# A whole network on one core: its order is planned anew, with measured durations and a time to landing for each kind of DMA

## The chip, the cores and the metric

The kernel runs on one core of a Trainium2 chip. The time is the device time of one execution in microseconds (us); a profiled execution also has a span, from its first to its last instruction. Engines: PE (TensorE, matrix products), DVE (VectorE), ACT (ScalarE), POOL (GpSimd) and SP (SyncE), which issues all DMAs here.

## What the kernel computes

The input is a batch of 8 images of 32 channels of 256 x 256 points, in fp32. Four layers follow each other; each one adds to x a function of the group-normalised x (16 groups of two channels):

```python
x = x + _L0_conv_ref(_gn(x), L0_conv_conv_w, L0_conv_conv_b)
x = x + _L1_conv_ref(_gn(x), L1_conv_weight)
x = x + _L2_conv_ref(_gn(x), L2_conv_weight, L2_conv_bias)
x = x + _L3_conv_ref(_gn(x), ...)
```

Layer 0 is a 1 x 1 convolution, followed by a depthwise 5 x 5 convolution whose 25 taps per channel are a pooled 5 x 5 picture of that same result. Layer 1 quantises x and w to 8 bits and takes minus the sum of |patch - w| over 32 channels and 3 x 3 places, for each of 32 output channels. Layer 2 is an ordinary 3 x 3 convolution. Layer 3 cuts the image into windows of 8 x 8, normalises over channels, and passes the result through four small networks: k1, k2 and k3 side by side (on three arrangements of the window), their sum through k4. Each of them is

```python
def _fastkan(x, ln_g, ln_b, ws, wb, bb):
    ln = _layernorm(x, ln_g, ln_b)
    basis = jnp.exp(-((ln[..., None] - GRID) / DENOM) ** 2)
    flat = basis.reshape(*basis.shape[:-2], -1)
    return flat @ ws.T + jax.nn.silu(x) @ wb.T + bb
```

with a grid of 8 points: eight squares and eight exponentials of every element.

## The kernel before

**The work.** A tile has 128 partitions: 4 blocks of rows of the image times 32 channels. An image has 8 chunks of 128 x 2048 values (F = 2048).

- `stage0` (layer 0): loads x by chunks for the sums and the pooled picture (the DMA at L821, sums on DVE at L828 to L834, squares on ACT at L721), then takes the taps on PE (L1084 for image 0; `one_block`, L1012, for the other images), and stores x1. A last walk loads x1 (L1144), scales it on ACT (L1151), rounds it on DVE (L1157, L1158) and stores it as bf16 integers q (L1162).
- `stage1` (layer 1): an image goes in two halves; the half's q is loaded into `qh` (L1231). A half has 16 passes of two output channels. A pass needs 18 distances max(q - w, 0) (2 channels x 9 taps) of 128 x 32 x 258 values. DVE makes them (L1186, one instruction for 8256 values), and where ACT is free it makes the first `RA` rows of one or all of it (L1188). They go to one of two buffers `dv`; PE sums each over the channels into `psA` (L1204, 288 products a pass). When a pass is done, ACT evicts psA (the gate, L1283), 256 times in all: 8 images x 2 halves x 16 passes.
- `stage2` (layer 2): 8 chunks; a load of x2 (L1327 to L1340), a normalisation on ACT (L1345), 9 taps on PE (L1362), an eviction on ACT (L1378) and a store of x3 (L1386).
- `stage3` (layer 3): each of 8 chunks goes through four kan passes (`kan`, 256 in all): centring on PE (L678), an eviction (L1458 on ACT or L1463 on DVE), its square (L1466 on ACT or L1467 on DVE), the variance on PE (L1475), logarithm and exponential for the root on ACT (L1488, L1492), broadcasts on PE (L1507), a product on DVE (L1515); then eight squares (L1611 on ACT or L1616 on DVE), eight exponentials on ACT (L1626), eight main products on PE (L678), one product with silu of the input, and an eviction on ACT (L1699). The input and its silu go through HBM to change their arrangement: stores y, yd, sy, syd, sz (L1543; L1548 in eight DMAs), loads at L1567, L1569, L1588 and L1591, the sums oa and od (stored at L1708, loaded at L1658 and L1662, the latter in sixteen DMAs). ACT uses two tables, one for logarithm and exponential, one for silu; a switch is an instruction of its own (L1805).

**What sets the order.** Nothing of it is written out by hand. Each stage calls `plan.add` with an engine, a duration in us, what it reads and writes, and a rank. `Plan.run` (L263) then walks through time like a scheduler: whenever an engine is free it takes, of the tasks whose inputs are ready and whose buffers fit, the one of the lowest rank; distances and their sums on PE are fillers that an engine takes where nothing else is (`fill`, L389; `piece`, L428; on PE, `on_pe` takes them first when enough have queued up). The list in which tasks were taken is then emitted, and each engine works through its part of it strictly in order. So the planner's durations are never executed: they only decide the order of the instructions and which buffer each one gets. On the chip, an instruction waits for what it needs, and all behind it on its engine wait too.

**What the planner takes a DMA to cost.** SP is busy for the task's duration (often 2.0 us, or 0.5 us for a single DMA); its data arrive when one shared mover has moved all kilobytes before them, at 210 KB per us:

```python
busy[e] = now + us
mover = max(mover, now + us) + t.kb / 210.0
t.end = mover
```

A task that reads the data is ready 2.0 us after that (`LAT["SP"]`), a buffer that a DMA has read is free after 0.5 us.

**Constants.** `room()` divides 41,280 words a partition: three places for `si` (operands of stage 3's last products), two for `dv`, small ones, `NX` fixed places of 3072 words for `x0` (chunks of stages 0 and 2), and the rest in one piece, `sb`: 20,992 words, from which everything else takes what it needs (a chunk of stage 3 takes 2048). With NX = 0, x0 comes from sb too, and only while 6400 words (`WIDE_SPARE`) stay free besides; the first tasks of a kan pass leave `SPARE` words free. `IDLE` says per image how long ACT must have been idle before it takes a distance. When all distances are done (`over()`), squares and evictions may go to DVE as well as to ACT (`.other`). `HOLDT` is the number of the exponential that must be done before a kan pass starts its main products in that last part, `SWITCH` the rank that a table switch costs, `SUMS` when a half's sums of q are taken. `TURN`, `L0A`, `L0B`, `L2A`, `L3A` and `L3B` place the steps of the stages among the ranks, by image; layer 1's pass has the rank of its number, so that, for instance, `L3A[b]` says how far into the next image's layer 1 the layer 3 of image b begins.

Of the kernel before, what the change touches and what calls it, by code (L numbers as in the profile page):

```python
# [13 lines left out]
AF = mybir.ActivationFunctionType  # L14
# [55 lines left out]
NX = 0  # L70
NBAS, NSI = 0, 3
TURN = (
    (0.6962, -0.3, -0.2033, 1.3419, 0.9756, -0.0716, 0.0444, 0.123, 0.0689, 0.1702, 0.1109, -0.1569, 0.9648, 0.4157),
    (0.4978, -0.3, -0.0103, 0.9164, 1.1185, -0.0225, 0.0583, 0.81, 0.1545, 0.2437, 0.1558, -0.1941, 0.9648, 1.2236),
# [12 lines left out]
IDLE = (4.0, 2.0, 8.0, 8.0, 1000.0, 16.0, 8.0, 8.0)  # L87
NDV = 2
SPARE = 1792
# [3 lines left out]
HOLDT = 4  # L93
HOLD = 1
SUMS = 1.314
RA = 4
HALVES = 0
SWITCH = 0.006
L0A = (0.5664, -0.1509, 0.3344, 0.396, 0.4459, 0.5225, 0.5225)
L0B = (1.2, 0.9692, 1.0696, 0.2501, 0.4205, 0.2211, 0.5807)  # L100
L2A = (-0.4443, 0.2719, 0.2484, 0.4, -0.0809, 0.0425, 0.3641, 0.335)
L3A = (0.3139, 0.6, 0.5451, 0.5786, -0.4733, 0.6, 0.5806, 0.0117)
L3B = (0.3712, 0.937, 0.2, 0.3674, 0.2077, 0.8294, 0.444, 0.2665)
# [12 lines left out]
NI = 4  # L116
# [21 lines left out]
class Plan:  # L138
# [4 lines left out]
    LAT = {"PE": 0.15, "DVE": 0.14, "ACT": 0.2, "SP": 2.0}  # L143
# [13 lines left out]
    def add(self, eng, us, fn, r=(), w=(), rank=0.0, after=(), table=None, spare=0, kb=0, acc=()):  # L157
        t = Task()
        t.eng, t.us, t.fn, t.rank, t.table, t.spare, t.kb = eng, us, fn, rank, table, spare, kb
        t.n, t.gate, t.other = len(self.tasks), None, None  # L160
# [102 lines left out]
    def run(self):  # L263
# [4 lines left out]
        table, mover = None, 0.0  # L268
        count = 0
# [17 lines left out]
        while left or any(not p.done for p in self.passes):  # L287
            moved = True
            while moved:
                moved = False  # L290
                for e in engines:
# [34 lines left out]
                    if t.table in (LN_EXP, SILU):  # L326
                        if table != t.table:
                            t.load = table = t.table
                            us += 1.29
                    t.start = now  # L330
                    order.append(t)
                    if e == "SP":
                        busy[e] = now + us
                        mover = max(mover, now + us) + t.kb / 210.0
                        t.end = mover
                    else:
                        busy[e] = t.end = now + us
                        if e == "ACT" and t.n is not None:
                            self.idle = t.end
# [7 lines left out]
            while events and events[0][0] <= now + 1e-9:  # L347
# [3 lines left out]
                elif what == 2:  # L351
                    t.over = True
                    left -= t.n is not None
                    heapq.heappush(events, (t.end + (0.5 if t.eng == "SP" else self.LAT[t.eng]), 3, count, t))
# [53 lines left out]
class Pass:  # L408
# [19 lines left out]
    def piece(self, plan, e):  # L428
# [32 lines left out]
        us = (0.13 + 1.075 * (hi - lo) / 16) if e == "DVE" else 0.12 + 3.575 * (hi - lo) / 16  # L461
# [41 lines left out]
def kernel(  # L503
# [180 lines left out]
    class Norm:  # L684
# [23 lines left out]
        def add_squares(self, src, at, i, size, rank, first=None):  # L708

            if not self.chunks & 1 << i:  # L710
                self.chunks |= 1 << i
                plan.add(
                    "DVE", 0.16,
# [6 lines left out]
                "ACT", 0.18 + 0.8365e-3 * size,  # L720
# [7 lines left out]
        def finish(self):  # L728
# [14 lines left out]
            plan.add("DVE", 1.1 if n == 1 else 1.5, first, r=[*self.bufs, self.summed], w=[small], rank=self.rank)  # L743
# [11 lines left out]
            plan.add("DVE", 0.5, second, r=[p], w=[small], rank=self.rank)  # L755
# [22 lines left out]
            plan.add("DVE", 2.8, third, r=[p], w=[small] + out, rank=self.rank)  # L778
# [30 lines left out]
    def stage0(b, rank, span, after):  # L809
# [8 lines left out]
        for k in range(NCH):  # L818
            xt = Buf("x0", XW)
            plan.add(  # L820
                "SP", 2.0, lambda k=k, xt=xt: by_block(lambda p, q: nc.sync.dma_start(sb(xt, F)[p], xn[k, q])),  # L821
                w=[xt], rank=r(0.02 * k), after=after, kb=1024,
# [14 lines left out]
            plan.add("DVE", 2.95, pool, r=[xt], w=[rs_buf[k], norm.summed], rank=r(0.02 * k))  # L837
# [35 lines left out]
        plan.add("DVE", 2.6, parts, r=rs_buf, w=[sm["c1"]], rank=r(0.2))  # L873
# [35 lines left out]
        plan.add("DVE", 2.6, diag, r=[p, sm["c0"]], w=[sm["diag"], sm["c1"]], rank=r(0.22))  # L909
# [26 lines left out]
        plan.add("DVE", 1.8, taps, r=[p, sm["w0f"]], w=[sm["diag"], sm["c1"]], rank=r(0.22))  # L936
# [15 lines left out]
        if b:  # L952
            plan.add("DVE", 1.6, pairs, r=[sm["diag"]], w=[sm["w4"]], rank=r(0.22))
# [8 lines left out]
        def paired_chunk(k):  # L962
            for i in range(2):
# [5 lines left out]
                    "SP", 2.0, lambda i=i, xo=xo: store_chunk(k, xo, 2 * i, 2 * i + 2), r=[xo], acc=[x1buf[k]],  # L969
                    rank=rk, kb=512,  # L970
                )

        def one_block(k, half, xo):
# [27 lines left out]
            if first(0) == 0 or first(1) + R == H:  # L1001
                plan.add("DVE", 0.6, clear, w=[xt], rank=rk - 0.03 * span, after=after)
            plan.add("SP", 2.0, load, w=[xt], rank=rk - 0.03 * span, kb=1536, after=after)
# [29 lines left out]
            for t in [K + mid] + [t for t in range(3 * K) if t != K + mid]:  # L1033
# [3 lines left out]
                "ACT", 1.0,  # L1037
# [7 lines left out]
        for k in range(NCH):  # L1045
# [6 lines left out]
            def load(k=k, xt=xt):  # L1052
# [9 lines left out]
                "SP", 2.0, load, w=[xt], rank=rk - 0.03 * span, after=prev[-2:-1] or [*norm.done.writers], kb=1536  # L1062
# [62 lines left out]
            plan.add("SP", 2.0, lambda k=k, xt=xt: store_chunk(k, xt), r=[xt], w=[x1buf[k]], rank=rk, kb=1024)  # L1125
# [13 lines left out]
        for k in range(NCH):  # L1139
# [3 lines left out]
                "SP", 0.5,  # L1143
# [4 lines left out]
                r=[x1buf[k]], w=[t], rank=rk, after=norm1.done.writers, kb=1024,  # L1148
# [6 lines left out]
            def clip(t=t):  # L1155
# [6 lines left out]
                "SP", 2.0, lambda k=k, t=t: by_block(lambda p, q: nc.sync.dma_start(qd[k, q], q16(t)[p])),  # L1162
                r=[t], w=[qbuf[k]], rank=rk, kb=512,
# [56 lines left out]
    def stage1(b, x1buf, qbuf):  # L1220
# [3 lines left out]
        for h in range(NH):  # L1224
# [14 lines left out]
            for part, (k0, k1) in enumerate(((h * NI - 1, h * NI + 2), (h * NI + 1, (h + 1) * NI + 1))):  # L1239
                loads.append(plan.add(  # L1240
                    "SP", 2.0, lambda load=load, part=part: load(part), r=[qbuf[k % NCH] for k in range(k0, k1)], w=[qh_buf[part]],
                    rank=b - 0.5 + 0.5 * h, kb=1150,
# [18 lines left out]
            for g in range(NG):  # L1261
# [8 lines left out]
                if ends:  # L1270
# [7 lines left out]
                    "SP", 0.5, lambda spot=spot, ours=ours: nc.sync.dma_start(ours(), spot("x1")),  # L1278
# [656 lines left out]
```

## Time and profile before

| | us |
|---|---|
| three runs, median (lowest to highest) | 14384.8 (14374.49 to 14384.93) |
| the profiled execution: its own time | 14384.95 |
| its span | 14383.0 |
| from the span's start to the first distance (L1186) | 436 |
| from there to the last gate (L1283) | 12270 |
| from there to the end | 1670 |
| distances on DVE (L1186), busy in all | 10162.9 and 266.5 (into dv and into sb) |
| exponentials and squares on ACT with the largest sums (L1626, L1611) | 3177.3, 3338.1 |

The page of a profile gives busy times, the span in 40 slices, the chain that ended last and the costliest groups of instructions. Other views of the same trace answer questions: busy time of each engine in a stretch of the span (columns: stretch, length, then busy us and number of instructions of PE, PEld, DVE, ACT and POOL, the granted clock of TensorE, the DMA engines' share, GB/s), who waited for whom (sum, times, longest), and the timeline (start, length, engine, line, operation, output<-input, number; in brackets the idle time just before and what ended it). A group's mean is that of one instruction; where instructions overlap a little, the sum of a group is larger than the time it filled.

### The profile page before, as it was taken

The numbers are of one execution on the slowest core, as the hardware profiler recorded it, in microseconds if no ns is written. First come the engines' busy times: TensorE is split into PE (matmuls) and PEld (weight loads), VectorE is DVE, ScalarE is ACT, GpSimd is POOL, SyncE is SP. The second block draws the span as 40 slices with busy tenths as digits, with TensorE's granted clock in tenths as the row PEclk, the third lists the DMA queues.
The fourth block names the chain that finished last, engine by engine and source line by source line (L and its number), as shares of the span: only waits on it lengthen the run. The fifth ranks groups of instructions, "written<-read, shape, count | busy, mean of one in ns | idle before, by whom it ended". The sixth has DMA issues, their size and how long they took to land. (4 is left out here: it accounts for less than half of the span.)

```text
span 14383.0 us, 505334 instructions
## 1 busy us (share of the span) xinstructions
PE 12186.8 (85%) x235861; PEld 4033.4 (28%) x236108; DVE 12668.2 (88%) x8013; ACT 11538.2 (80%) x7730; POOL 45.6 (0%) x23
## 2 busy tenths in 40 slices
PE   6797988998899889988899987999888887766666
PEld 4232322222222222222222222222222222222222
DVE  1899998888999999999998899979999999965776
ACT  1566679888688887888888888888988888877777
POOL 0000000000000000000000000000000000000000
PEclk9898999999999999999999999999999999987777
DMA  4434346565666656665666557565554545556665
GB/s 93 118 74 109 95 140 167 145 150 147 172 151 153 170 143 162 151 147 153 162 150 152 147 155 164 147 157 147 159 122 123 144 123 121 130 147 165 155 166 133
DMA packets 2259381, 2052.45 MB, mean 143 GB/s; under 512 B 1418240, under 2 KB 1897472, under 8 KB 2168192
## 3 DMA queue, kind: packets, MB, share of 16 engines
q1 hardware_dynamic: 2257280, 2020.11, 55.8%
q8 instruction: 1847, 30.26, 0.9%
q14 instruction: 254, 2.08, 0.1%
HBM read 1247.93 MB, written 771.75 MB: 140 GB/s over the span
## 5 line engine op out<-in xcount | busy, mean ns | idle before, releaser
L1186 DVE TENSOR_SCALAR dv<-qh,w1q 128x8256 bf16<-128x8256 bf16 (+4 forms) x4914 | 10162.9, 2132 | 539.2 <-PE psA L1204 524.4
L1204 PE MATMUL psA<-dv,sel_b 128*32 128x512 bf16 x70824 | 4894.9, 391 | 843.3 <-DVE dv L1186 752.4
L1611 ACT ACTIVATE arena<-arena,kb 128x2048 f32<-128x2048 f32 x1687 | 3338.1, 1993 | 285.3 <-DVE arena L1515 214.7
L1204 PEld LDWEIGHTS <-sel_b 128*32 128x32 bf16 x73728 | 1834.1, 97 | 5238.8 <-issue 4052.9
L1626 ACT ACTIVATE arena<-arena 128x2048 f32<-128x2048 f32 x1687 | 3177.3, 1899 | 0.6
L678 PE MATMUL psB<-arena,tl 32*32 32x512 f32 x67568 | 2578.5, 620 | 341.3 <-ACT arena L1626 160.0
L1012 PE MATMUL psC<-arena,w 64*32 64x510 f32 (+2 forms) x26880 | 1757.9, 598 | 27.9 <-issue 17.2
L678 PEld LDWEIGHTS psB<-arena,tl 32*32 32x32 f32 x67568 | 696.2, 104 | 1449.3 <-issue 587.4
L1515 DVE TENSOR_TENSOR arena<-psB,arena 128x2048 f32<-128x2048 f32 (+1 forms) x296 | 659.0, 2226 | 160.5 <-PE psB L1507 130.4
L1699 ACT ACTIVATE si<-psB,cols_sb 128x2048 f32<-128x2048 f32 x181 | 355.3, 1963 | 358.8 <-PE psB L678 348.9
L1012 PEld LDWEIGHTS psC<-arena,w 64*32 64x32 f32 x26880 | 377.6, 105 | 912.4 <-issue 871.6
L678 PE MATMUL psB<-si,tl 32*32 32x512 f32 x13840 | 582.4, 616 | 49.8 <-issue 16.7
L1362 PE MATMUL psB<-arena,tl 32*32 32x510 f32 (+3 forms) x16384 | 613.4, 612 | 9.1 <-issue 8.9
L1188 ACT ACTIVATE dv<-qh,w1n 128x1032 bf16<-128x1032 bf16 (+2 forms) x173 | 338.2, 1974 | 351.0 <-PE psA L1204 339.0
L1458 ACT ACTIVATE arena<-psB 128x2048 f32<-128x2048 f32 (+1 forms) x223 | 413.1, 1852 | 255.8 <-PE psB L678 253.2
L1616 DVE SCALAR_TENSOR_TENSOR arena<-arena,kb 128x2048 f32<-128x2048 f32 x247 | 566.2, 2345 | 30.1 <-PE psB L678 17.5
L1188 ACT ACTIVATE arena<-qh,w1n 128x1032 bf16<-128x1032 bf16 (+3 forms) x167 | 519.2, 3162 | 71.1 <-PE psA L1204 65.4
L1466 ACT ACTIVATE arena<-arena 128x2048 f32<-128x2048 f32 x274 | 524.1, 1913 | 8.1 <-PE psV L1475 0.3
L1507 PE MATMUL psB<-rs,tl 32*32 32x512 f32 x9216 | 386.2, 664 | 148.1 <-DVE arena L1515 74.8
L1626 ACT ACTIVATE arena<-arena,kbsq 128x2048 f32<-128x2048 f32 x247 | 478.9, 1989 | 6.2 <-DVE arena L1616 6.1
L1475 PE MATMUL psV<-arena,tl 128*32 128x512 f32 x2560 | 379.8, 663 | 113.9 <-DVE arena L1467 59.2
L1283 ACT ACTIVATE xr<-psA,wsum 128x512 f32<-128x512 f32 x256 | 173.3, 677 | 226.9 <-PE psA L1204 197.0
(192 smaller groups left out, 7206.3 us busy)
## 6 DMA issues: line engine op xcount, KB each, us to landing
arena<-x SPq DMA_DIRECT2D x192, 1024.0 KB
arena<-in_x_dram SPq DMA_DIRECT2D x450, 384.0 KB
arena<-y SPq DMA_DIRECT2D x128, 1024.0 KB
si<-sy SPq DMA_DIRECT2D x472, 256.0 KB
arena<-in_x_dram SPq DMA_DIRECT2D x256, 256.0 KB
xr<-x SPq DMA_DIRECT2D x256, 256.0 KB
x<-xr SPq DMA_DIRECT2D x256, 256.0 KB
x<-arena SPq DMA_DIRECT2D x64, 1024.0 KB
```

The source lines that it names most:

```text
L678: nc.tensor.matmul(view(o[j * C : (j + 1) * C, i - first, :]), w_, src(rows, i, j), start=start, stop=stop)
L1012: nc.tensor.matmul(o[:, :, c0:c1], w4[rows, t, :], grid(rows)[:, 2 * j + y : 2 * j + y + 2, c0 + dx : c1 + dx], start=t == K + mid, stop=F ...
L1186: nc.vector.tensor_scalar(dst, src, w1q[:, at : at + 1], 0.0, ALU.subtract, ALU.max)
L1188: nc.scalar.activation(dst, src, AF.Relu, bias=w1n[:, at : at + 1])
L1204: nc.tensor.matmul(psA[j * C : (j + 1) * C, :], sel_b[:, w, :], v, start=start, stop=stop)
L1362: nc.tensor.matmul(o[:, lo - 2 * j : hi - 2 * j, c0:c1], (wc if t == 4 else tl[:, W2T + t, :])[rows], d[rows, lo + dy + 1 : hi + dy + 1, c ...
L1458: lambda ps=ps, at=at: nc.scalar.activation(sb(c)[:, at], ps().rearrange("p s f -> p (s f)"), func, bias=shift),
L1466: square = plan.add("ACT", 1.82, lambda: nc.scalar.activation(sb(sq), sb(c), AF.Square), r=[c], w=[sq], rank=rk)
L1515: lambda ps=ps, at=at: nc.vector.tensor_tensor(sb(c)[:, at], ps().rearrange("p s f -> p (s f)"), sb(c)[:, at], ALU.mult),
L1611: lambda: nc.scalar.activation(sb(bas), sb(rb), AF.Square, bias=kb[:, n, k : k + 1]),
L1616: nc.vector.scalar_tensor_tensor(sb(bas), sb(rb), kb2[:, n, k : k + 1], sb(rb), ALU.add, ALU.mult)
L1626: lambda: nc.scalar.activation(sb(bas), sb(bas), AF.Exp, scale=-1.0, bias=0.0 if sq.eng == "ACT" else kbsq[:, n, k : k + 1]),
```

## The change

The planner gets other costs, a DMA gets another model, one buffer place is fixed, and the ranks have other values. No stage computes anything differently.

The DMA's model: a task now brings the number n of its DMAs and a time to landing; SP spends us / n on each, at most eight (`AHEAD`) may be under way, and the data are there when the last has landed and the mover, now at 250 KB per us, has done its share. The additional 2.0 us before a reader is ready become 0.1 us, and so does the 0.5 us before the buffer is free.

```diff
-NX = 0
+NX = 1
...
-IDLE = (4.0, 2.0, 8.0, 8.0, 1000.0, 16.0, 8.0, 8.0)
+IDLE = (4.0, 4.0, 1000.0, 16.0, 8.0, 4.0, 4.0, 1000.0)
...
-SPARE = 1792
+SPARE = 3584
...
-HOLDT = 4
+HOLDT = 3
...
-SUMS = 1.314
-RA = 4
+SUMS = 1.233
+RA = 8
...
-SWITCH = 0.006
-L0A = (0.5664, -0.1509, 0.3344, 0.396, 0.4459, 0.5225, 0.5225)
-L0B = (1.2, 0.9692, 1.0696, 0.2501, 0.4205, 0.2211, 0.5807)
-L2A = (-0.4443, 0.2719, 0.2484, 0.4, -0.0809, 0.0425, 0.3641, 0.335)
-L3A = (0.3139, 0.6, 0.5451, 0.5786, -0.4733, 0.6, 0.5806, 0.0117)
-L3B = (0.3712, 0.937, 0.2, 0.3674, 0.2077, 0.8294, 0.444, 0.2665)
+SWITCH = 0.003
+L0A = (0.0873, 0.48, 0.1425, 0.6, 0.6, 0.6, 0.6)
+L0B = (0.2881, 0.9706, 0.6607, 0.5229, 0.4614, 0.5856, 0.9604)
+L2A = (-0.2794, 0.2943, 0.2943, 0.2943, 0.4, 0.2943, 0.3674, 0.3674)
+L3A = (0.6, 0.6, 0.494, 0.0926, 0.6, 0.54, 0.6, 0.6)
+L3B = (0.439, 0.858, 0.4492, 0.9385, 0.3346, 0.972, 0.6761, 0.7473)
...
-    LAT = {"PE": 0.15, "DVE": 0.14, "ACT": 0.2, "SP": 2.0}
+    LAT = {"PE": 0.15, "DVE": 0.14, "ACT": 0.2, "SP": 0.1}
+    RATE, AHEAD = 250.0, 8
...
+        landed = [0.0] * self.AHEAD
...
                     if e == "SP":
-                        busy[e] = now + us
-                        mover = max(mover, now + us) + t.kb / 210.0
-                        t.end = mover
+                        at, (n, land) = now, t.dma
+                        for _ in range(n):
+                            at = max(at, landed.pop(0)) + us / n
+                            landed.append(at + land)
+                        busy[e] = at
+                        mover = max(mover, now) + t.kb / self.RATE
+                        t.end = max(mover, at + land)
+                        landed[-1] = t.end
...
-                    heapq.heappush(events, (t.end + (0.5 if t.eng == "SP" else self.LAT[t.eng]), 3, count, t))
+                    heapq.heappush(events, (t.end + self.LAT[t.eng], 3, count, t))
```

`TURN`, the places of layer 3's fourteen steps, changes in nearly all its values. The durations in the calls change one by one; some of them (n and time to landing in the added pair):

| task | us before | us after | DMAs, time to landing |
|---|---|---|---|
| ACT piece of a distance, 4 rows before, 8 after | 1.01 | 1.91 | |
| gate L1283 | 0.57 | 0.665 | |
| load of x for stage 0, L821 | 2.0 | 1.75 | 4, 6.5 |
| load of qh, L1231 | 2.0 | 1.95 | 4, 9.5 |
| load of x2 for stage 2, L1327 to L1340 | 6.0 | 1.6 | 3, 5.2 |
| store yd or syd, L1548 | 4.0 | 9.0 | 8, 3.0 |
| load of y or yd, L1567, L1569 | 0.5 | 0.36 | 1, 5.3 |
| load of oa, L1658 | 2.0 | 2.0 | 4, 6.8 |
| load of od, L1662 | 8.0 | 13.3 | 16, 2.0 |
| table switch | 1.29 | 1.283 | |

Of the durations on PE, DVE and ACT most change by under 0.2 us, some small ones by up to 1.0 us (the `diag` step of stage 0, 2.6 to 1.62).

## The prediction

> **What bounds the kernel now.** I read the page first, then the busy time by stretches of the span, then who waited for whom, then the timeline around the longest idle times. The page says that three engines are nearly full, and slices tell where:
>
> ```profile
> span 14383.0 us, 505334 instructions
> ...
> PE 12186.8 (85%) x235861; PEld 4033.4 (28%) x236108; DVE 12668.2 (88%) x8013; ACT 11538.2 (80%) x7730; POOL 45.6 (0%) x23
> ...
> DVE  1899998888999999999998899979999999965776
> ACT  1566679888688887888888888888988888877777
> ```
>
> DVE is at 8 and 9 from the second slice to the thirty-fourth and drops in the last six. I cut the span into a head (0 to 436 us, before the first L1186), sixteen half-images of layer 1 (each ended by the sixteenth gate L1283 of its half), and a tail (from 12706 us). Four of those eighteen stretches:
>
> ```profile
> core 0: us, PE busy (x) PEld busy (x) DVE busy (x) ACT busy (x) POOL busy (x), PEclk, DMA share, GB/s
> 2412.00:3303.00 891.00, 840.48 (x16115) 250.49 (x16132) 716.58 (x360) 787.34 (x539) 1.27 (x1) 0.98 0.61 147
> 8848.00:9702.00 854.00, 805.59 (x15521) 241.42 (x15536) 734.80 (x417) 734.72 (x507) 1.34 (x1) 0.99 0.62 151
> 11228.00:11974.00 746.00, 631.92 (x12834) 205.94 (x12818) 711.67 (x424) 632.06 (x424) 0.95 (x1) 0.97 0.48 126
> 12706.00:14376.00 1670.00, 1108.40 (x22242) 424.71 (x22242) 1101.52 (x614) 1247.45 (x747) 0.00 (x0) 0.76 0.62 156
> ```
>
> Third row, a normal half: DVE idles 746 - 712 = 34 us, it is the bound. First and second rows (halves 3 and 11): DVE idles 174 and 119 us while ACT has 787 and 735 us of work; ACT is the bound there. ACT never idles less than about 90 us in a half: 104, 92, 93, 95 and 90 us in halves 3, 5, 7, 9 and 13. DVE idles 28, 33, 27, 26, 34 and 21 us in halves 5, 6, 8, 13, 14 and 15. So I read a half as the larger of DVE + 30 (6 in halves 0 and 1) and ACT + 95. Summed with the loads below this gives 12263 us for the sixteen halves; they took 12270. The waits say how DVE gets stuck: it waits for a dv slot that PE has not yet read, and PE stands in order behind stage 3's work.
>
> ```profile
> DVE dv L1186 <- PE psA L1204: 524.4, 438, 32.8
> ```
>
> The tail is different: nothing is full (DVE 66%, ACT 75%). Six times from 13637 to 14243 us ACT waits 10.7 to 12.4 us before an eviction L1699, 70 us in all, and the timeline shows why:
>
> ```profile
> 14078.28 16.06 SPq L1662 DMA_DIRECT2D si<-od  x16
> 14094.45 0.53 SPq L1567 DMA_DIRECT2D arena<-yd  x1
> 14095.10 2.28 SPq L1588 DMA_DIRECT2D dv<-sy  x4
> ```
> ```profile
> 14107.96 1.99 ACT L1626 ACTIVATE arena<-arena,kbsq 128x2048 f32<-128x2048 f32 x1
> 14122.14 1.97 ACT L1699 ACTIVATE dv<-psB,cols_sb 128x2048 f32<-128x2048 f32 x1 [12.19 <-issue]
> ```
>
> The sy load stands behind sixteen issues that keep SP for 16 us; the planner of before charges them 8.0.
>
> **The change, part by part.** No instruction's work changes; the planner's costs, one buffer slot, the piece size and the priorities do, and the order on every engine comes out new. What can be costed is the load that the new order puts in each stretch: I cut both orders at the same gates and gave each instruction the mean time of its group in the trace, without overlaps (a distance of 6192 or 2064 elements, which before does not have, between its neighbours on the same line).
>
> *Totals.* ACT 11631 us before, 11633 after; DVE 12668 and 12641. ACT's distance pieces become 4 to 8 rows per step (RA), 340 pieces become 339, their elements 925,704 and 910,224: 15,480 elements more for DVE, at (2363 - 1292) / 4128 = 0.26 ns each 4 us. DVE gets 44 pieces more; the fixed part of one is 2363 - 8256 x 0.26 = 220 ns, so 10 us. Fourteen squares L1616 leave DVE (-14 x 2.35 = -33 us), eight squares L1467 (-8 x 2.29 = -18 us), and seven half evictions L1463 come (+9 us): -28 us, as the totals say. Twelve table loads fewer (217 to 205): 12 x 1.28 = -15 us of ACT, in the totals already. So the sum of work is worth nothing; what counts is where it lies.
>
> The table-load row is `x217 | 278.4, 1283`, with 3.8 us of idle time ahead of all 217. The Trainium skill (ScalarE: Activation LUTs, What ACT_TABLE_LOAD costs) adds a drain of about 1380 ns to each switch, 2.66 us in all; by it the twelve would be worth 32 us. The trace has no such drain, so the row decides.
>
> *The sixteen halves* (us; span of before, then DVE and ACT load before, and after; last, the change of the larger of DVE + 30 and ACT + 95):
>
> ```
> half span  DVE ACT  after DVE ACT  change
> 0    588   585 478        596 488    +11
> 1    613   611 447        619 442     +8
> 2    775   730 582        750 595    +20
> 3    891   714 796        713 671   -125
> 4    802   768 630        770 602     +2
> 5    753   722 667        716 679    +12
> 6    797   763 653        771 678     +8
> 7    783   728 699        734 751    +52
> 8    794   767 682        765 729    +27
> 9    799   716 712        720 703     -9
> 10   818   764 706        767 711     +5
> 11   855   732 744        713 705    -39
> 12   785   745 681        736 695    +14
> 13   741   715 655        714 672    +17
> 14   745   712 638        722 678    +31
> 15   733   713 640        716 666    +18
> ```
>
> Halves 3 and 11 are relieved, because image 1's ACT takes fewer distances (IDLE 2.0 to 4.0) and stage 3 of image 0 starts later (L3A 0.31 to 0.6). What left them comes back in 7, 8 and 12 to 15. Sum +53 us. By single passes instead of halves, counting in each of the 255 passes the larger of ACT and DVE, the sum goes from 11842 to 11729: -113 us, because passes with ACT more than 5 us above DVE go from 27 to 14. The first reading says that a lump is carried over neighbours, the second that it isn't. The truth lies between; half 3 of before shows single stalls of up to 32.8 us, so lumps do hurt. I take the middle, **-30 us**.
>
> *The head.* PE's order up to the first distance is the same. On SP the second load of qh, which both DVE and ACT wait for at 436 us, stands behind 8 loads of the next image's x instead of 20; the last twelve took 8.52 us to issue (0.71 us each): about **-8 us**. It can't be much more, since that load also waits for the last store of q, issued at 409 us. The 9 us of DVE work on those loads (L828 to L834) move behind the first distance and are in half 0's +11.
>
> *The tail.* 48 kan passes instead of 50 are left after the last gate. ACT + DVE load: 1220 + 1101 = 2321 before, 1166 + 1047 = 2213 after. At the same idle share 1670 x 2213 / 2321 = 1592: -78 us. Least: one of the two lay beside stage 2 of the last image, where ACT is 62 to 82% busy, and counts nothing; 40 passes followed the last stage 2 eviction (in 1248 us, 31 us each), now 39: -31 us. Most: the 12 us waits vanish too. SP's order does not change (od's sixteen issues still stand ahead of yd and sy), but in ACT's order six operations now stand between the two evictions where one stood: four exponentials, a square, the table load and silu, 4 x 1.90 + 1.99 + 1.28 + 1.91 = 12.8 us against 2.0. That covers about 10.8 of each 12 us in five of six chunks. Covered work only counts if nothing else is late next: after the roots, ACT waits another 6.7 us for L1515 in each chunk, and that stays. So -78 to -78 - 72 = -150. I take **-110**, the middle.
>
> *One slot for x0, SPARE doubled.* A fixed slot of 3072 words leaves 17,920 words instead of 20,992 for the tiles of 2048: 8 instead of 10. During stages 0 and 2 nothing changes (they took such a tile from there anyway). In the tail's last 1250 us, two exponentials fewer can run ahead. No row shows that price; below: nothing, if the loads of the table, which are those of the order made with the slot, can start when they stand; above: a wait of 6.7 us like that for L1515, once more in each of 8 chunks, +54. I take nothing, since the squares and exponentials stand as far ahead of their evictions as before (see the 12.8 us), and keep +54 in the range.
>
> *Landing times and eight DMAs in flight* only alter the order. The plan's load of y is 5.3 us; the trace has one that took 11.02 us on the final chain:
>
> ```profile
> 14150.28 11.02 DMA arena<-y
> ```
>
> The Trainium skill (DMA: Bandwidth & Descriptors, Latency and other measured facts) has HBM's access latency at 0.2 us on average and 2 us at high load; that speaks against one number per kind. The trace's DMA share goes from 0.33 (436 to 1024 us) to 0.62 in the tail, so load does vary here.
>
> **Sum.** -8 - 30 - 110 = -148 us. The profiled execution took 14384.95 us (span 14383.0), the median of the three runs is 14384.8, so the base is the same: 14385 - 148 = **14237 us**, 1.0% faster.
>
> **Rivals.**
> 1. *Every lump hurts and the waits are covered*: -8 - 113 - 150 = -271, 14114 us. For it: the 32.8 us stalls; against it: ACT's 90 us of idle time per half hardly vary.
> 2. *ACT becomes the bound of the main part*: in halves 7, 8 and 12 to 15 its load rises by 14 to 52 us, and passes 118, 120 and 121 have 53, 59 and 73 us of ACT beside 41 to 46 of DVE. Price +53; with the head's -8 it ends slower than before as soon as the tail gains less than 45 us. With the slot's +54 against the tail's least gain of 31, 14385 - 8 + 53 + 23 = 14453 us. Against it: ACT's idle time includes waits that a truer plan may shorten.
> 3. *The change doesn't do what it says*: the order moves, the stalls only change places, head -8, halves +53, tail between its -31 and -78: 14352 to 14399, about 14380 us, within 0.2%.
>
> **Chances.** Forecast 0.50, rival 1 0.20, rival 2 0.20, rival 3 0.10. A measurement of this kernel tells about 0.2%, 29 us, from no change: faster 0.70, same 0.10, slower 0.20. Range: down to rival 1's 14115; up to 14440, into rival 2's.
>
> **What would show it.** Right: DVE's idle time in half 3 falls from 174 to under 60 us; half 7 is no longer than 815 us; the tail takes about 1560 us, and L1699's waits of 12 us are gone from its chunks. Wrong: halves 7, 8 and 12 to 15 all grow by their changes above (rival 2), the tail stays above 1640 us, or ACT waits for memory, seen as long idle time before L1611 or for a DMA.

## The result, and the profile after

The changed kernel takes **14118.2 us** (median of four runs, 14110.88 to 14126.86) against 14381.7 us for the kernel before in the same series: a ratio of 0.9818, 95% interval 0.9801 to 0.9835, so 263 us or 1.8% less. The forecast was 14237, the range reached down to 14115. Its profiled execution took 14121.4 us, with a span of 14119.5.

The same lines of the page as those of before:

```profile
span 14119.5 us, 505388 instructions
...
PE 12117.6 (86%) x235858; PEld 3981.8 (28%) x236108; DVE 12640.6 (90%) x8042; ACT 11552.4 (82%) x7732; POOL 14.5 (0%) x23
...
DVE  1899999999999999988989999999999999995777
ACT  1677678897688887899789888898899889987887
```

The work hardly differs (DVE -28 us, ACT +14 us, and as many products on PE), so the 263 us went out of waits. PE's busy time falls by 69 us; the mean granted clock is 0.950 where it was 0.940, and these runs don't show which of clock and waits follows from the other. DVE has four low slices at the end (5777) where five stood (65776; I had read six). The lines move by 8 in the changed kernel (L1186 is L1194, L1283 is L1291, L1699 is L1707). The same four stretches, halves 3, 11 and 14 and the tail, busy time by engine:

```profile
core 0: us, PE busy (x) PEld busy (x) DVE busy (x) ACT busy (x) POOL busy (x), PEclk, DMA share, GB/s
2436.00:3187.00 751.00, 730.79 (x14129) 217.19 (x14136) 712.82 (x351) 663.61 (x458) 0.30 (x1) 1.00 0.62 152
8836.00:9609.00 773.00, 745.78 (x14520) 222.73 (x14520) 714.67 (x352) 697.39 (x478) 0.35 (x2) 1.00 0.63 153
11137.00:11884.00 747.00, 639.06 (x13191) 209.97 (x13209) 722.58 (x429) 669.39 (x448) 1.22 (x1) 0.99 0.55 145
12619.00:14113.00 1494.00, 1037.90 (x21354) 393.89 (x21322) 1042.90 (x592) 1191.90 (x712) 0.00 (x0) 0.79 0.65 165
```

Half 3 lost 124 us of ACT's work and 140 us of length; DVE idles 751 - 713 = 38 us in it, where it idled 174. In half 14 ACT now idles 747 - 669 = 78 us: less than the 90 that I had taken for a floor. DVE's wait for a slot of dv, 524.4 us before, moved little:

```profile
DVE dv L1194 <- PE psA L1212: 485.7, 477, 34.1
```

By stretches (us; a pass is one kan pass, counted by its eviction L1699 or L1707 after the last gate; the tail ends with the last of these, and the 6 to 7 us of the final store behind it are in no column):

| | head | sixteen halves | tail | passes in it | us a pass |
|---|---|---|---|---|---|
| before | 436 | 12270 | 1670 | 50 | 33.4 |
| after | 413 | 12206 | 1493 | 48 | 31.1 |
| change | -23 | -64 | -176 | | |
| predicted | -8 | -30 | -110 | 48 | |

### The profile page after: what moved, and what is told of

Read it like the earlier page. It is cut to its first block, busy times and chain, and to the rows that moved or that the text cites. A ratio compares the mean times of both kernels' runs of the same rounds, so it can differ in the third digit from the quotient of the medians.

```text
span 14119.5 us, 505388 instructions
## 1 busy us (share of the span) xinstructions
PE 12117.6 (86%) x235858; PEld 3981.8 (28%) x236108; DVE 12640.6 (90%) x8042; ACT 11552.4 (82%) x7732; POOL 14.5 (0%) x23
## 5 line engine op out<-in xcount | busy, mean ns | idle before, releaser
L1194 DVE TENSOR_SCALAR dv<-qh,w1q 128x8256 bf16<-128x8256 bf16 (+4 forms) x4940 | 10182.6, 2128 | 501.7 <-PE psA L1212 485.7
L1619 ACT ACTIVATE arena<-arena,kb 128x2048 f32<-128x2048 f32 x1701 | 3374.8, 1997 | 343.4 <-DVE arena L1523 195.3
L1634 ACT ACTIVATE arena<-arena 128x2048 f32<-128x2048 f32 x1701 | 3211.1, 1903 | 0.5
L1020 PE MATMUL psC<-x,w 64*32 64x510 f32 (+2 forms) x13680 | 900.1, 597 | 6.8 <-issue 5.8
L1020 PE MATMUL psC<-arena,w 64*32 64x508 f32 (+2 forms) x13200 | 872.0, 598 | 17.5 <-issue 11.9
L1196 ACT ACTIVATE dv<-qh,w1n 128x2064 bf16<-128x2064 bf16 (+1 forms) x179 | 406.0, 2284 | 325.8 <-PE psA L1212 311.7
L686 PE MATMUL psB<-si,tl 32*32 32x512 f32 x13872 | 566.1, 610 | 34.6 <-issue 12.7
L1707 ACT ACTIVATE si<-psB,cols_sb 128x2048 f32<-128x2048 f32 x185 | 363.5, 1965 | 271.0 <-PE psB L686 254.6
L1474 ACT ACTIVATE arena<-arena 128x2048 f32<-128x2048 f32 x282 | 539.8, 1914 | 13.1 <-DVE arena L1471 5.2
L1515 PE MATMUL psB<-rs,tl 32*32 32x512 f32 x9328 | 391.3, 651 | 143.6 <-DVE arena L1523 56.8
L1624 DVE SCALAR_TENSOR_TENSOR arena<-arena,kb 128x2048 f32<-128x2048 f32 x208 | 478.6, 2348 | 27.6 <-PE psB L686 23.9
L1196 ACT ACTIVATE arena<-qh,w1n 128x2064 bf16<-128x2064 bf16 (+1 forms) x160 | 443.1, 2803 | 69.0 <-PE psA L1212 63.9
L1634 ACT ACTIVATE arena<-arena,kbsq 128x2048 f32<-128x2048 f32 x208 | 404.8, 1992 | 0.2 <-DVE arena L1624 0.2
L686 PE MATMUL psB<-dv,tl 32*32 32x512 f32 x4480 | 239.7, 795 | 181.1 <-ACT si L1707 71.0
L1370 PE MATMUL psB<-arena,tl 32*32 32x510 f32 (+2 forms) x9728 | 363.3, 606 | 8.7 <-issue 8.7
```

Of the source, the lines that this page charges most:

```text
L686: nc.tensor.matmul(view(o[j * C : (j + 1) * C, i - first, :]), w_, src(rows, i, j), start=start, stop=stop)
L1020: nc.tensor.matmul(o[:, :, c0:c1], w4[rows, t, :], grid(rows)[:, 2 * j + y : 2 * j + y + 2, c0 + dx : c1 + dx], start=t == K + mid, stop=F ...
L1194: nc.vector.tensor_scalar(dst, src, w1q[:, at : at + 1], 0.0, ALU.subtract, ALU.max)
L1196: nc.scalar.activation(dst, src, AF.Relu, bias=w1n[:, at : at + 1])
L1474: square = plan.add("ACT", 1.82, lambda: nc.scalar.activation(sb(sq), sb(c), AF.Square), r=[c], w=[sq], rank=rk)
L1515: nc.tensor.matmul(ps()[g * C : (g + 1) * C, i - first, :], tl[rows, BC + 4 * n + g, :], sb(rs, FS)[rows], start=True, stop=True,)
```

## The experiments

My theory from here on: no single part is worth the 263 us. The truer costs and the new priorities gain together, since priorities found for one set of costs make lumps (stretches in which one engine has much more work than the others) with another. Truer the costs are in most places, not in all: the eight stores of a yd or syd take SP 9.7 us on average (4.0 in the old costs, 9.0 in the new), the gate 0.68 us (0.57 and 0.665), but the sixteen loads of an od 10.6 us (8.0 and 13.3). In e3's trace, which times them, loads of yd, y and oa land after 6.2, 8.3 and 6.7 us (medians); the new plan has 5.3, 5.3 and 6.8. The rivals: the costs alone make it; one setting makes it (the x0 slot, IDLE and RA, the constants of the last image); it is one lucky order; and, for the tail, SP's sixteen issues of od.

All experiments by the same stretches (each ratio is to the kernel before in its own series):

| | time, us | ratio to before, interval | head | halves | tail | passes | us a pass |
|---|---|---|---|---|---|---|---|
| e1 new costs, old priorities | 14295.6 | 0.9943 (0.9928 to 0.9958) | 418 | 12326 | 1537 | 46 | 33.4 |
| e2 after, no x0 slot | 14693.6 | 1.0218 (1.0203 to 1.0234) | 414 | 13045 | 1233 | 37 | 33.3 |
| e3 before, od on GpSimd | 14406.6 | 1.0020 (1.0011 to 1.0030) | 432 | 12302 | 1667 | 50 | 33.3 |
| e4 after, od on GpSimd | 14155.4 | 0.9842 (0.9826 to 0.9859) | 411 | 12249 | 1497 | 48 | 31.2 |
| e5 before, new last image | 14429.4 | 1.0042 (1.0027 to 1.0057) | 431 | 12267 | 1728 | 50 | 34.6 |
| e6 before, new IDLE and RA | 14555.8 | 1.0127 (1.0112 to 1.0142) | 424 | 12345 | 1759 | 54 | 32.6 |
| e7 before, x0 slot | 14589.0 | 1.0154 (1.0139 to 1.0170) | 430 | 12468 | 1697 | 50 | 33.9 |
| e8 after, SWITCH 0.0025 | 14113.8 | 0.9823 (0.9807 to 0.9839) | 414 | 12198 | 1490 | 48 | 31.0 |
| e9 before, short chain | 14352.9 | 0.9984 (0.9975 to 0.9994) | 429 | 12257 | 1658 | 50 | 33.2 |
| e10 after, HOLDT 4 | 14120.9 | 0.9820 (0.9805 to 0.9835) | 414 | 12201 | 1499 | 48 | 31.2 |
| e11 after, 16 DMAs in flight | 14277.8 | 0.9929 (0.9915 to 0.9944) | 421 | 12310 | 1540 | 50 | 30.8 |
| e12 e1, new last image | 14220.2 | 0.9888 (0.9871 to 0.9904) | 411 | 12336 | 1469 | 46 | 31.9 |

None is measurably faster than the changed kernel (e8 has its very order, see there).

### e1: the new costs with the old priorities

In the changed kernel:

```diff
-NX, TURN, IDLE, SPARE, HOLDT, SUMS, RA, SWITCH, L0A to L3B of after
+NX, TURN, IDLE, SPARE, HOLDT, SUMS, RA, SWITCH, L0A to L3B of before
```

> The changed kernel's durations, landing times and eight DMAs in flight, with the priorities and settings of before (NX, TURN, IDLE, SPARE, HOLDT, SUMS, RA, SWITCH, L0A to L3B). Theory (costs and search work together; the priorities of before were found for the old costs, and lumps of ACT work come from IDLE, RA and L3A): the head stays at about 436 us, half 3 stays long with DVE idle above 100 us, the tail gains part; 14280 to 14400 us. Rival A (truer costs alone make the gain, the search only fits them): 14120 to 14170 us. Rival B (any plan that was not searched with its own costs is bad): above 14450 us.

Measured: 14295.6 us, in the theory's range and out of both rivals'. The costs alone are worth 80 of the 263 us. The head falls to 418, against the expectation; the tail gains 133 us, all by four passes fewer at the same 33.4 us each; the halves take those passes and grow by 55. Half 3 keeps its lump (ACT 824 us, DVE idle 906 - 728 = 178):

```profile
2432.00:3338.00 906.00, 834.73 (x16326) 250.53 (x16327) 728.17 (x387) 824.30 (x556) 1.27 (x1) 0.97 0.62 152
```

So half 3's relief and the shorter pass come only with new priorities. The other corner, all the new priorities on the old costs, has no kernel to measure: there the planner stops with tasks left over that it can't place. The same holds for SPARE, TURN, RA or IDLE alone.

### e2 and e7: the x0 slot, taken away and alone

e2 in the changed kernel; e7 does the reverse in the kernel before:

```diff
-NX = 1
+NX = 0
```

> The changed kernel without the fixed x0 slot (NX 0), all else as changed. Theory: the slot's worth is the head, where the first x chunk need not wait for a place that the weight preparation holds (first pooling at 25.8 instead of 32.8 us): 7 to 15 us more, 14125 to 14135 us, and noise of the new order on top, within 14100 to 14170. Rival A (the slot makes memory scarce in the tail, as the prediction's 0 to +54 had it): 14065 to 14110 us. Rival B (the slot is a large part of the gain, because loads of the next image's x no longer fight for the arena during the halves): 14200 us or more.

> The kernel before with the fixed x0 slot (NX 1) alone. Theory (the slot keeps the next image's first layer from starving for memory, which only the priorities searched with it let come near; the order of before doesn't starve): first pooling at about 26 instead of 32.8 us, the head 2 to 8 us shorter, the tail 0 to 54 us longer for two tiles fewer: 14370 to 14430 us. Rival A (the slot by itself is worth hundreds of us, as the run without it might say): 14200 us or less. Rival B (a plan with less memory starves elsewhere): above 14500 us.

e2 takes 14693.6 us, 575 more than the changed kernel: rival B by the number, and near it in kind. But the slot is no gain by itself: in e7 it costs 217 us. Most of e2's loss lies in half 14 (1510 us instead of 747); half 9 loses another 156 us, and the other halves together gain 80. Half 14's busy times, and DVE's longest waits in it:

```profile
11221.00:12731.00 1510.00, 1045.44 (x19983) 337.37 (x20000) 794.74 (x498) 1326.73 (x819) 1.28 (x1) 0.83 0.53 135
```
```profile
DVE arena L1523 <- PE psB L1515: 400.3, 17, 84.3
DVE arena L1165 <- ACT arena L1159: 193.2, 7, 75.1
```

DVE works 795 us of it, ACT 1327. The half cannot begin, because the last image's q (L1165, eight steps from 11390 to 11963 us) isn't there. The last image's layer 0 (its evictions, L1046) ended at 11237 us; in the changed kernel it ended at 9758, and the last step of its q began at 10072. ACT runs kan passes meanwhile, so the tail has only 37 left (1233 us), which gives 260 us back. So with these priorities the slot keeps the next image's layer 0 from starving. That it starves for memory fits the code (without the slot x0 must find its 3072 words beside 6400 free ones), but nothing here shows memory by itself.

In e7 the first chunk is pooled at 26.2 us instead of 33.0, much as in the changed kernel (26.1), and yet the head is 429.9 us long, against 429.1 to 436.1 in the four kernels that keep the order of before in the head. So the early chunk is worth a few us at most. The halves lose 198 us, the tail 27; half 12 alone goes from 785 to 889 us, with DVE busy for 747.

### e3 and e4: od's loads off SP's queue

The same edit in the kernel before and in the changed one; no other instruction moves:

```diff
-                                nc.sync.dma_start(
+                                nc.gpsimd.dma_start(
                                     dst[:, q * FS : (q + 1) * FS]...
```

> The kernel before with the same order, only the sixteen od loads (L1662) issued by GpSimd's queue instead of SP's. Theory (the 16 us that SP takes to issue them set the six waits of 10.7 to 12.4 us before L1699): those waits fall under 3 us and the tail loses 40 to 75 us: 14305 to 14345 us. Rival A (the waits are filled by the next wait, that of 6.7 us for L1515 or for PE): 14360 to 14385 us. Rival B (GpSimd issues slower and the loads land later, so others wait): 14400 us or more.

> The changed kernel with the same order, only the sixteen od loads (L1670) issued by GpSimd's queue. Theory (the new order of ACT already covers SP's 16 us; only waits of 8.4 and 12.3 us are left, and the 6.7 us for L1523 does not hang on it): 10 to 25 us less, 14093 to 14108 us. Rival A (SP still sets the pace of the steady chunks, 121 to 114 us per four passes): 40 to 80 us less, 14040 to 14080 us. Rival B (GpSimd is slower): 14130 us or more.

The theory falls in both. With the od issues gone, SP issues yd 41 us ahead of the eviction instead of 28; but sy leaves at the same point as before, 27 us ahead of it, and SP stands idle until then. And the waits stay, 10.7 to 12.0 us in all six places. SP and ACT in e3:

```profile
14106.55 0.38 SPq L1567 DMA_DIRECT2D arena<-yd  x1
14120.55 1.78 SPq L1588 DMA_DIRECT2D dv<-sy  x4
```
```profile
14132.30 1.94 ACT L1699 ACTIVATE si<-psB,cols_sb 128x2048 f32<-128x2048 f32 x1
14134.15 1.99 ACT L1626 ACTIVATE arena<-arena,kbsq 128x2048 f32<-128x2048 f32 x1
14147.89 1.97 ACT L1699 ACTIVATE dv<-psB,cols_sb 128x2048 f32<-128x2048 f32 x1 [11.75 <-issue]
```

So SP's 16 us neither held the sy load nor set these waits: they lay beside them. The changed kernel still spends 15.47 us on such an issue (at 14051 us) without such a wait. The tails stay within 4 us; both kernels lose in the halves (+31 and +43 us), more than the up to 13 us by which the halves of one order differ between profiles. GpSimd's median issue is as short as SP's (584 and 607 ns), but 228 of the 1024 in e3 take over 2 us, up to 27.4, which makes the mean 1094 ns against SP's 661. All 228 lie in the halves; in the tail no issue of GpSimd's takes over 0.6 us. The edit also changes the transfers: they go out as 32,768 packets, where SP's were some 278,500. DVE's waits for dv grow by 20 us in e3 (524.4 to 544.5) and by 40 in e4 (485.7 to 525.2). Which of these makes the loss, the runs don't show. The Trainium skill (Trainium Kernel Development and Optimization, Key Constraints) says that issuing from several engines saves the issuing queue's time and nothing else, since all run on the same DMA engines; here that time was not what anything waited for, and the move cost 31 and 37 us.

### e9: a shorter chain of matmuls

```diff
-lambda bas=bases[k]: mm16(psB, ...
+lambda bas=bases[k]: last and 2 <= k < 6 or mm16(psB, ...
```

> The kernel before in the same order, with four of the eight basis matmul groups (k 2 to 5, 16 matmuls each) left out of every kan pass of the last image: its output lacks these terms. Theory (the six waits of 10.7 to 12.4 us before L1699 are the length of the next pass's own chain of matmuls: it can begin only when the eviction before it has emptied psB, and ACT has nothing else in its queue): each wait falls by about 4 x 1.1 us to 6 to 8.5 us, and the tail by 25 to 60 us: 14310 to 14350 us. Rival A (a load that lands late, or SP's issues, set the end of the chain): the waits stay within 1.5 us of what they were and the time within 15 us of 14376.

Measured: 14352.9 us, 19 us less than before in the same series (14371.9), between the two. The tail's part is 12 us (1670 to 1658), less than the theory's 25. Four of the six waits fall, by 1.2 to 4.0 us: 12.25, 11.70, 10.81 and 12.19 become 9.35, 9.54, 9.62 and 8.24 us; the other two, 12.38 and 10.72, stay (11.85, 11.42). First the chain's beginning and end on PE in the kernel before (from the eviction at 14106 to that at 14122), then PE and ACT between two evictions of e9 (some of PE's rows left out, marked by dots):

```profile
14108.11 2.42 PE L678 MATMUL psB<-dv,tl 32*32 32x512 f32 x32
...
14120.43 1.63 PE L678 MATMUL psB<-dv,tl 32*32 32x512 f32 x23
```
```profile
13956.43 2.11 PE L678 MATMUL psB<-dv,tl 32*32 32x512 f32 x32
13958.14 2.38 PE L678 MATMUL psB<-arena,tl 32*32 32x512 f32 x32
13959.84 2.21 PE L678 MATMUL psC<-arena,tl 32*32 32x512 f32 x16
13963.48 0.66 PE L678 MATMUL psC<-arena,tl 32*32 32x512 f32 x8 [1.43 <-DVE arena L1463]
...
13966.17 1.63 PE L678 MATMUL psB<-dv,tl 32*32 32x512 f32 x29
```
```profile
13954.43 1.95 ACT L1699 ACTIVATE si<-psB,cols_sb 128x2048 f32<-128x2048 f32 x1
13956.28 1.99 ACT L1626 ACTIVATE arena<-arena,kbsq 128x2048 f32<-128x2048 f32 x1
13967.89 1.97 ACT L1699 ACTIVATE dv<-psB,cols_sb 128x2048 f32<-128x2048 f32 x1 [9.62 <-issue]
```

The eviction at 13954 empties psB; PE begins the next pass's chain at 13956 and ends it just ahead of 13967.9. In the kernel before the chain has nine groups of 32 matmul records and lasts 14 us without a pause; with four groups (some 4.4 us) left out, it lasts 11.4 us: PE waits 1.4 us within it for DVE, and its centring products (psC) stand in between. So in these four places the wait is the time that PE takes for the next chain, since psB is one accumulator and the next instruction in ACT's order is the eviction that waits for it; how long that is depends on PE's own waits too. In the other two places e9's trace names PE's psB as well, but there PE itself waits within the shorter chain: in the last place 2.59 us for DVE's square (L1467), before a variance (L1475) that stands ahead of the chain's last groups. That these two waits follow the number of matmuls isn't shown.

What the new order does is put work there. ACT in the changed kernel between the same two evictions of a chunk (the last two ahead of the silu L1556, here L1564):

```profile
13860.30 1.97 ACT L1707 ACTIVATE si<-psB,cols_sb 128x2048 f32<-128x2048 f32 x1 [1.16 <-PE psB L686]
13862.17 1.99 ACT L1634 ACTIVATE dv<-dv,kbsq 128x2048 f32<-128x2048 f32 x1
13864.06 2.00 ACT L1634 ACTIVATE arena<-arena,kbsq 128x2048 f32<-128x2048 f32 x1
13867.63 2.00 ACT L1619 ACTIVATE arena<-arena,kb 128x2048 f32<-128x2048 f32 x1 [1.57 <-PE psB L686]
13869.54 1.99 ACT L1634 ACTIVATE dv<-dv,kbsq 128x2048 f32<-128x2048 f32 x1
13871.43 1.89 ACT L1634 ACTIVATE arena<-arena 128x2048 f32<-128x2048 f32 x1
13873.34 1.28 ACT L1813 ACT_TABLE_LOAD   x1
13874.64 1.91 ACT L1731 ACTIVATE si<-si 128x2048 f32<-128x2048 f32 x1
13876.46 1.95 ACT L1707 ACTIVATE arena<-psB,cols_sb 128x2048 f32<-128x2048 f32 x1
```

The time from eviction to eviction is the same, 16.2 us (16.0 before). But ACT spends it on four exponentials, a square, the table load and a silu, and is idle for 1.6 us of it instead of 12.2.

### e5, e10 and e12: which constants set the tail's pace

The first two lines are e5 (in the kernel before) and e12 (in e1), the others e10 (in the changed kernel):

```diff
-TURN[1], HOLDT 4, last entries of L2A, L3A and L3B of before
+TURN[1], HOLDT 3, last entries of L2A, L3A and L3B of after
...
-HOLDT = 3
+HOLDT = 4
```

> The kernel before (its costs and landing model), with the changed kernel's constants for the last image alone: HOLDT 3, TURN's second row, and the last entries of L2A, L3A and L3B. Theory (the tail's gain comes from the truer costs first, 133 of 176 us by the run with new costs and old priorities, and these constants add the rest): head and halves as before, tail 1610 to 1670 us, 14310 to 14385 us in all. Rival A (the priorities of the last image make the tail's gain): tail 1500 to 1560 us, 14200 to 14270 us. Rival B (priorities that were searched for other costs spoil the plan): 14420 us or more.

> The changed kernel with HOLDT 4 instead of 3: on each engine the order is the same up to the last passes of the tail, where a pass's chain of matmuls may begin only when the fifth of its exponentials is done, not the fourth. Theory (the exponentials that still stand behind the start of the chain are what covers it on ACT; one fewer, 1.9 us, in each of some 36 passes, of which a half is exposed): 25 to 70 us more, 14143 to 14190 us, and waits of 2 to 6 us come back before L1707. Rival A (other work fills the time): within 12 us of 14118. Rival B (the chain then stalls less in its middle): 14060 to 14105 us.

> The kernel with the new costs and the old priorities (14295.6 us; last gate at 12743.6, 46 passes left in 1537 us, 126 us for four passes in the steady part), and on top the changed kernel's constants for the last image (TURN's second row, HOLDT 3, the last entries of L2A, L3A and L3B). On each engine the order is the same up to the tail. Theory (the tail's pace needs both: the old costs with these constants gave 34.6 us a pass, the new costs with the old constants 33.4, both new 31.1): 114 us for four passes instead of 126, 46 passes at 31.1 us, 1430 us of tail, 14170 to 14215 us in all. Rival A (the pace comes from the whole new plan, what is left ready at the last gate among it): tail 1500 us or more, 14260 to 14310 us. Rival B (constants searched with another rest spoil the tail): above 14320 us.

HOLDT makes no difference to the time (14120.9 against 14118.2 us): rival A, and the waits before L1707 hardly differ, so my picture of the start of the chain was wrong. It is no clean test, though: the order departs from the changed kernel's at the start of the tail, not in its last passes. The other two fill a square of four, us a pass:

| | old constants of the last image | new |
|---|---|---|
| old costs | 33.4 (before) | 34.6 (e5) |
| new costs | 33.4 (e1) | 31.9 (e12) |

Neither shortens the pass alone, both together do. In the steady part four passes take 121 us before, 133 in e5, 126 in e1, 113 in e12 and 114 in the changed kernel (the last three distances between the silus L1556 or L1564 of neighbouring chunks; the one before these took 126 us in e12). e5 is slower than its theory had it, even: rival B. e12's tail of 1469 us lies between theory (1430) and rival A (1500), its time 5 us above the theory's range; the pace of the steady part is what the theory said.

The three runs also split the gain: the new costs alone give 80 us (e1), the last image's constants on top another 75 (e12), and all other settings the last 102 us. These last come from the halves (12336 to 12206); the tail grows by 24 us, with two passes more left to it.

### e6: IDLE and RA alone

```diff
-IDLE = (4.0, 2.0, 8.0, 8.0, 1000.0, 16.0, 8.0, 8.0)
+IDLE = (4.0, 4.0, 1000.0, 16.0, 8.0, 4.0, 4.0, 1000.0)
-RA = 4
+RA = 8
```

> The kernel before with two settings of the changed kernel, IDLE (image 1 from 2.0 to 4.0 us, and other images) and RA (ACT's distance pieces up to 8 rows). Theory (ACT's lump in half 3 is made by IDLE of image 1; ACT takes fewer distances there): DVE's idle time in half 3 falls from 174 to under 80 us and the half from 891 to under 810 us, other halves move by up to 30 us either way, the tail stays: 14280 to 14360 us. Rival A (half 3's lump is stage 3 of image 0, which L3A sets): half 3 stays at 870 to 900 us and the total within 30 us of 14376. Rival B (settings not searched with their costs spoil the plan): 14420 us or more.

Half 3 does what the theory said: 806 us, ACT 715 instead of 787, DVE idle 93 instead of 174 (expected: under 80). The whole does what rival B said: 14555.8 us. Half 11 loses 92 us too, but halves 8, 9, 12 and 14 grow by 35 to 59 us, and 54 passes are left for a tail of 1759 us.

```profile
2398.00:3205.00 807.00, 780.11 (x15054) 231.13 (x15054) 714.38 (x358) 714.92 (x493) 0.30 (x1) 0.99 0.63 151
```

Here a lump is moved by two settings, and what they give there is taken elsewhere.

### e8: a repeat

```diff
-SWITCH = 0.003
+SWITCH = 0.0025
```

> The changed kernel with SWITCH 0.0025 instead of 0.003: one priority constant moved by a sixth, nothing else. It measures how much of the result hangs on this one plan. Theory (truer costs make the plans good in general, head and tail mostly): 14120 to 14260 us. Rival (the search found one lucky order; a near miss loses it): above 14300 us, with one or two halves that stall by 100 us or more as in the run without the slot.

The plan comes out the same, instruction for instruction, so this says nothing on luck: it is a second measurement of the changed order, 14113.8 against 14118.2 us, 0.03% apart.

### e11: no limit on DMAs in flight

```diff
-    RATE, AHEAD = 250.0, 8
+    RATE, AHEAD = 250.0, 16
```

> The changed kernel with 16 DMAs in flight in the plan instead of 8 (the same order as with 1000: no limit), all else as changed; the plan of the whole main part comes out anew. Theory (the limit of eight holds back few transfers, and a plan that was not searched with its own costs loses by its lumps, as those before did): 14150 to 14400 us, one or two halves with 100 us of idle DVE or more. Rival A (the limit is what makes the plan true): above 14400 us, with DVE or PE waiting for DMAs. Rival B (it matters neither way): 14100 to 14140 us.

The order is new from the first image on, and 160 us slower: the theory. In half 9 (855 us) DVE idles 122 us. It keeps the new pace in the tail (30.8 us a pass) but leaves 50 passes to it, and its halves are 104 us longer. So the tail's pace outlives a different order of everything before it; the halves' part of the gain doesn't.

## Why the prediction was right in direction and short in size

The total came out at rival 1's 14114, but not by rival 1's terms: it had -8, -113 and -150, measured were -23, -64 and -176. Its number is no proof of its reason.

- **Head**: -8 predicted, -23 measured (the head of before varies by 7 us between kernels with its order, 432 on average over four, so -19 is the better figure). The step that failed is the bound: "it can't be much more, since that load also waits for the last store of q". SP's queue shows that the last store moved too, before and after:

```profile
409.14 1.76 SPq L1162 DMA_DIRECT2D q<-arena  x4
411.00 8.52 SPq L821 DMA_DIRECT2D arena<-in_x_dram  x12
420.29 3.62 SPq L1231 DMA_DIRECT2D qh<-q  x4
```
```profile
394.48 1.79 SPq L1170 DMA_DIRECT2D q<-arena  x4
396.38 2.36 SPq L829 DMA_DIRECT2D arena<-in_x_dram  x4
398.80 2.17 SPq L1239 DMA_DIRECT2D qh<-q  x4
```

  Twelve x loads ahead of the qh load did go, as said (those between the last store and it take 2.4 us instead of 8.5); the last store of q came 15 us earlier on top. The new costs with the old priorities and no slot have it too (load of qh at 403.7 in e1; heads of 418 and 411 us in e1 and e12), and e2 without the slot has a head of 414: so it is the costs, not the slot.
- **Halves**: the sign was right in 15 of 16, though four of these moved by no more than 3 us, which is noise. The size was close in halves 3 (-140, said -125) and 7 (+57, +52) and too small in 8 (+52, +27), 9 (-33, -9) and 11 (-82, -39). The mis-sized term is "ACT + 95": in halves 12 to 15, where it gave +14 to +31, they grew by 1 to 3 us. ACT idles 71 to 78 us in halves 9, 11, 13, 14 and 15 now, so the 95 was waits of a plan, not a property of the half. Halves 12 to 15 account for some 70 of the 117 us between the +53 of that reading and the -64 measured. The middle between the two readings, -30, was a choice and not a reason. (The table's ACT column counts the head's 78 us in half 0 and its DVE column doesn't; DVE is the larger there either way.)
- **Tail**: -110 said, "-78 to -150" its bounds, -176 measured. What I had left out is the time beside the last image's stage 2: from the last gate to its last eviction it went from 421 to 359 us, and the same happened with the new costs alone (362 in e1). That is 62 of the 176 us. The other 114 lie behind it, 40 passes before and 39 after, where one pass less (31 us) and the covered waits (72) were to give 103 at most. The cover was right, to the operation (seven, not six, with the table load): in the chunk shown it took 10.6 us of ACT's idle time. But the 6.7 us waits for L1515 stayed, and a steady chunk became 7 us shorter. The waits of 11 to 12 us are gone from the steady chunks (two are left ahead of them, 8.4 and 12.3 us). The cause that I gave for these waits was wrong: the sixteen issues stand beside them (e3, e4), the chain on psB makes four of them (e9).
- **The x0 slot** at nothing, or up to +54 in the tail: most of its price lies elsewhere. With these priorities its lack costs 575 us, mostly in one half (e2); with the old ones its presence costs 217 us, of which the tail has 27 (e7).
- **Rivals 2 and 3**: halves 7 and 8 grew as rival 2 said, 12 to 15 didn't, and the tail gained far more than the 45 us from which it decides. Half 7 is 840 us long, above the 815 that I had named as the sign. DVE's 38 us of idle time in half 3 (under 60) came as said; the tail's 1493 us lie below the 1560.

What stays open: how much of the halves' 64 us is this one plan's luck. Five other plans, each with a part of the change (e1, e2, e6, e7, e11), lie between 12310 and 13045 us in the halves, all above the 12206 of the changed kernel and the 12270 of before; a plan found by another search with the new costs wasn't measured.

## What to carry to other kernels

When two things run side by side and end together, the trace shows both and names neither: before a queue is blamed for a wait, look at what the waiting instruction itself reads, here an accumulator that PE could fill only after the eviction before. A scheduler's costs and its priorities have to be judged together: the three parts of the new settings that could be put alone into the old plan lost 0.4 to 1.5%, and only the new costs gained by themselves (0.6%). Bound a step by events that the change can't move; the last store of q was none.

## What the runs showed of the hardware that was not expected

The same order measured in two series gave 14118.2 and 14113.8 us, and the head of one order still varied from 429.1 to 436.1 us between profiles. Moving 1024 loads of 64 KB from SP's queue to GpSimd's, with no other instruction in another order, cost 0.20% (0.11 to 0.30%), although SP was given back 0.66 us an issue. GpSimd's issues took 584 ns in the median, as short as SP's, but 228 of them, all in the halves, took over 2 us; 195 of these took 2.2 to 2.4 us, about as long as one of DVE's full distances there (2.36 us). Whether the two are linked, no run here shows.
